# Graph network on one core: the states of the edge loops leave from ScalarE's queue, one chunk later, instead of from SyncE's

## The chip, the cores and the metric

The kernel runs on one core of a Trainium2 chip. The metric is the time of one execution on the device, in microseconds (us). Three timed runs of the kernel before took 10173.44, 10185.69 and 10188.64 us; their median is 10185.69 us.

The engines are named as in the profile: PE is TensorE, DVE is VectorE, ACT is ScalarE, POOL is GpSimd and SP is SyncE. An engine that starts DMA transfers has a queue for that; in the profile `SPq` is SyncE's queue and `ACTq` ScalarE's. The memory from which tables are read and to which results go is the chip's DRAM; the tiles that engines work on lie in SBUF, and what PE writes lies in PSUM banks of 128 x 512 fp32.

## The reference

The input is a graph of 10000 nodes with 64 features and 160000 edges with 64 features. Each edge has a source and a destination, and the edges come sorted by destination. The reference applies two networks one after the other, each to a layer norm and ReLU of x, and adds the result to x.

The first has four softmax layers. Each gives every node a softmax over its incoming edges, feature by feature:

```python
m = relu(x[src] + ea) + EPS
logits = m * t
mx = segment_max(logits, dst)
e = exp(logits - mx[dst])
agg = segment_sum(m * e / segment_sum(e, dst)[dst], dst)
h = relu(layernorm((agg + x) @ W1 + b1)) @ W2 + b2
```

Here `ea` is the edges' features times a weight, the same in all four layers. The second network is one attention layer: a score per edge and head from K of the source, Q of the destination and E of the edge, clipped and put through exp, and a sum of V times the score over each node's edges.

## The kernel before

**How the work is tiled.** The edges are split into two halves of 80000. Features lie on the partitions: 64 partitions for the first half and 64 for the second, so one tile of 128 x 512 holds 512 edges of each half. Such a tile is a *chunk*. A half has 625 groups of 128 edges; 155 chunks have four groups, and the last three have two, two and one. Each of the five edge loops has 158 chunks.

**The stages** follow one another: encoding of the nodes (to about 115 us), softmax layer 0 (to 2010), then in turns a node layer (some 170 us) and softmax layers 1, 2 and 3 (2186 to 4005, 4172 to 6000, 6165 to 8000), a last node layer, the attention layer (8310 to 10150), and the final addition.

**A softmax layer** does not compute the maximum of each node first. It runs along the edges and carries a *state*: the running maximum `u`, the running sum of the exponentials `se` and the running sum of messages times exponentials `sm`. Each chunk's `se` and `sm` are written out to the DRAM tensor `st0` for every edge, and the node layer that follows gathers the row of each node's last edge from it. Chunk k passes these steps, with the line numbers of the profile:

- `fetch`, three chunks ahead, on SP: two loads of 64 KB with the marks of where a node's edges end (L797), and one load of 256 KB with the edges' features, transposed, from `eaT` (L766). In layer 0 the features come as rows (L773, L775), PE turns them (L784, L785), ACT copies the result (L788), and SP stores it to `eaT` for the later layers (L789).
- `front`: POOL gathers the source rows in 8 gathers (L756) into one of seven buffers `xg`. PE multiplies the features by their weight (L829) and adds the gathered rows (L831) in a bank `z`. ACT writes `lg` from it (L834, L835), DVE scans for the running maximum (L841) and subtracts it (L843), and ACT makes `up` and `e` (L846, L848, L849).
- `decay`: ACT makes `dec` from `up` (L856), in a single bank.
- `back`, one chunk later: DVE makes the messages (L869) and the scans `se` (L871) and `sm` (L874), transposes both into a tile `so` (L900), of which there are three, and SP issues four stores of 128 KB from it to `st0` (L904).

In layers 1 to 3 `z` takes turns in five banks, in layer 0 in three. Layer 0 also counts edges per node on DVE and PE (L468 to L477), and layer 1 clears a buffer in DRAM with one transfer of zeros every fourth chunk (L1131, on SP).

**The attention layer** has the same form. SP loads the queries (L1141), the marks and the features two chunks ahead. POOL gathers K and V in 8 gathers (L756). PE and DVE form the scores (L1180, L1183, L1185, L1191), ACT takes the exp (L1192), PE and DVE prepare the next chunk's queries (L1151 to L1160), and DVE scans the sums (L1201) and transposes them (L1212). SP stores them to `st1` in four stores of 64 KB (L1216).

**What sets the order.** `InOrder` ties every instruction to the one before it on its engine, so each engine works in the order of the program text. In an iteration k of a softmax loop that order is: the fetch of chunk k+3, the front of chunk k, the turning of chunk k+2 (layer 0 only), the counts (layer 0), the back of chunk k-1, and the decay of chunk k. On ACT it reads: `lg`, `lg`, `up`, `e`, `e`, in layer 0 the copy `ea` of chunk k+2, then `dec`. On SP it reads: marks, marks, `ea` of chunk k+3, then the four stores of chunk k-1.

**Waits of transfers.** Transfers of SP's and ACT's queues share eight completion semaphores in turn, in the order of the program. A transfer is issued only when the one eight before it has landed. POOL's gathers have eight of their own.

Of the kernel before, what the change touches and what calls it, by code (L numbers as in the profile page):

```python
# [26 lines left out]
def kernel(ctx: ExitStack, tc: tile.TileContext, a, out):  # L27
# [10 lines left out]
    nc = tc.nc  # L38
# [760 lines left out]

    V, S = nc.vector, nc.scalar  # L800

    def softmax_layer(l, ea_rows=None):

        prev = {}
        ph = ps("hist", [P, NT]) if ea_rows is not None else None
        per = 9
        if ph is not None:
            numbers = ps("oe", [P, P])
            V.tensor_copy(numbers, iota_row)
            nc.vector.tensor_scalar_mul(teps, tcol, EPS)  # L810

        def fetch(k):
            return load_marks(k, ends_d), load_ea(k) if ea_rows is None else load_rows(k, ea_rows)

        def z_bank(k):

            if ph is None and k % 5 > 2:
                return ps(("ept", "hist")[k % 5 - 3], [P, CE])
            return ps_a([P, CE])

        def front(k, marks, ea):
            g0, n, cols = span(k)
            m = n * G
            xg = edge.tile([P, CG, 2, D], F32, name="xg", bufs=7)
            for g in range(n):
                for s in range(2):
                    gather(xg[:, g, s, :], tables[l], index(g0 + g, s))
            z = z_bank(k)
            nc.tensor.matmul(z[:, :m], eencW, ea[:, :m], start=True, stop=False)  # L829
            for g in range(n):  # L830
                nc.tensor.matmul(z[:, g * G:(g + 1) * G], xg[:, g, :, :].rearrange("p s d -> p (s d)"),  # L831
                                 ident, start=False, stop=(g == n - 1))
            lg = ps("lg", [P, CE])
            S.activation(lg[:, :m], z[:, :m], AF.Relu)  # L834
            S.activation(lg[:, :m], lg[:, :m], AF.Identity, bias=teps[:, l:l + 1],  # L835
                         scale=tcol[:, l:l + 1])

            u = edge.tile([P, CE + 1], F32, name="u")
            last = prev.get("u", neg1)
            V.tensor_copy(u[:, 0:1], last)  # L840
            V.tensor_tensor_scan(u[:, 1:m + 1], lg[:, :m], marks[:, :m], last, op0=OP.max, op1=OP.add)  # L841
            prev["u"] = u[:, m:m + 1]
            V.tensor_sub(lg[:, :m], lg[:, :m], u[:, 0:m])  # L843

            up = edge.tile([P, CE], F32, name="up")
            S.activation(up[:, :m], lg[:, :m], AF.Relu)  # L846
            e = edge.tile([P, CE], F32, name="e")
            S.activation(e[:, :m], lg[:, :m], AF.Relu, scale=-1.0)  # L848
            S.activation(e[:, :m], e[:, :m], AF.Exp, scale=-1.0)  # L849
            return z, u, up, e  # L850

        def decay(k, up):
            g0, n, cols = span(k)
            m = n * G
            dec = ps("dec", [P, CE])
            S.activation(dec[:, :m], up[:, :m], AF.Exp, scale=-1.0)  # L856
            return dec

        def history(k):
            if ph is None:  # L860
                return []
            j0, j1 = min(k * per, R * KT), min((k + 1) * per, R * KT)
            return [count(edge, ph, j, min(j + 5, j1), numbers) for j in range(j0, j1, 5)]

        def back(k, z, u, dec, e):
            g0, n, cols = span(k)
            m = n * G
            me = edge.tile([P, CE], F32, name="me", bufs=1)
            V.scalar_tensor_tensor(me[:, :m], z[:, :m], 0.0, e[:, :m], op0=OP.max, op1=OP.mult)  # L869
            se = edge.tile([P, CE], F32, name="se")  # L870
            V.tensor_tensor_scan(se[:, :m], dec[:, :m], e[:, :m], prev.get("e", zero1),  # L871
                                 op0=OP.mult, op1=OP.add)
            sm = edge.tile([P, CE], F32, name="sm")
            V.tensor_tensor_scan(sm[:, :m], dec[:, :m], me[:, :m], prev.get("m", zero1),  # L874
                                 op0=OP.mult, op1=OP.add)
            prev["e"], prev["m"] = se[:, m - 1:m], sm[:, m - 1:m]
            if k == NC - 1:

                fin = edge.tile([P, 3], F32, name="fin", bufs=1)
                V.tensor_copy(fin[:, 0:1], u[:, m:m + 1])  # L880
                V.tensor_copy(fin[:, 1:2], se[:, m - 1:m])
                V.tensor_copy(fin[:, 2:3], sm[:, m - 1:m])
                pb = ps("oe", [D, 3])
                nc.tensor.matmul(pb, ident[:, D:], fin, start=True, stop=True)
                far = edge.tile([D, 3], F32, name="far", bufs=1)
                V.tensor_copy(far, pb)
                top = edge.tile([D, 4], F32, name="top", bufs=1)
                V.tensor_add(top[:, 0:1], far[:, 0:1], bothneg[:D, :])
                V.tensor_max(top[:, 1:2], top[:, 0:1], fin[:D, 0:1])
                V.tensor_sub(top[:, 2:3], fin[:D, 0:1], top[:, 1:2])  # L890
                V.tensor_sub(top[:, 3:4], top[:, 0:1], top[:, 1:2])
                S.activation(top[:, 2:4], top[:, 2:4], AF.Exp)
                for i, t in ((1, se), (2, sm)):
                    V.tensor_mul(far[:, i:i + 1], far[:, i:i + 1], top[:, 3:4])
                    V.scalar_tensor_tensor(t[:D, m - 1:m], fin[:D, i:i + 1], top[:, 2:3],
                                           far[:, i:i + 1], op0=OP.mult, op1=OP.add)

            so = edge.tile([P, CE // 32, 2, 32], F32, name="so", bufs=3)
            for i, t in ((0, se), (1, sm)):
                V.transpose(so[:, :m // 32, i, :], t[:, :m].rearrange("p (b e) -> p b e", e=32))  # L900
            rows_out = st0[2 * g0 * G:2 * (g0 + n) * G, :].rearrange(
                "(b e s) (h x) -> s h e b x", e=32, s=2, h=2)
            for q in range(4):
                nc.sync.dma_start(rows_out[q // 2, q % 2],  # L904
                                  so[q * 32:(q + 1) * 32, :m // 32].rearrange("p b i c -> p b (i c)"))

        order = InOrder()
        def columns_of(k):
            return got[k][1] if ea_rows is None else turn_rows(k, got[k][1])

        lead = 3
        got = [fetch(k) for k in range(lead)]
        eas = [columns_of(k) for k in range(2)]
        held, counts = None, []
        for k in range(NC):
            if k + lead < NC:
                got.append(fetch(k + lead))
            z, u, up, e = front(k, got[k][0], eas[k])
            if k + 2 < NC:
                eas.append(columns_of(k + 2))  # L920
            for c in counts:
                add_counts(*c)
            if counts and counts[-1][-1] == R * KT:
                rows_of_nodes(edge, ph)
            if held is not None:
                back(k - 1, *held)
            held = z, u, decay(k, up), e
            counts = history(k)
            if ph is not None:
                if 8 <= k < 8 + len(groups):  # L930
                    encode_columns(k - 8)
                if k == 8 + len(groups):
                    fold_weights()
            if l == 1 and k % 4 == 0:
                clear_queries(k // 4)
            order()
        back(NC - 1, *held)
        order()

    def node_layer(l):  # L940
# [193 lines left out]
    def attention_layer():  # L1134
# [60 lines left out]
        def back(k, keep, pv, sc):  # L1195
            g0, n, cols = span(k)
            m = n * G
# [6 lines left out]
            if k == NC - 1:  # L1204
# [6 lines left out]
            so = edge.tile([P, CE // 32, 32], F32, name="so1", tag="so", bufs=3)  # L1211
            V.transpose(so[:, :m // 32, :], s[:, :m].rearrange("p (b e) -> p b e", e=32))  # L1212
            rows_out = st1[2 * g0 * G:2 * (g0 + n) * G, :].rearrange(
                "(b e s) (h c) -> s h e b c", e=32, s=2, h=2)
            for q in range(4):
                nc.sync.dma_start(rows_out[q // 2, q % 2], so[q * 32:(q + 1) * 32, :m // 32])  # L1216

        order = InOrder()
        got = [fetch(k) for k in range(2)]
# [2 lines left out]
        for k in range(NC):  # L1222
            kvs = fetch_kv(k)
            if k + 2 < NC:
                got.append(fetch(k + 2))
            pv, psc = scores(k, kvs, made)
            if held is not None:
                back(k - 1, *held)
            held = got[k][0], pv, weights(k, psc)
            if k + 1 < NC:  # L1230
                made = ahead(k + 1, *got[k + 1])
            order()
        back(NC - 1, *held)
        order()

    puts = []
# [69 lines left out]
```

## Time and profile before

| what | value |
| --- | --- |
| timed runs, median (lowest to highest) | 10185.69 us (10173.44 to 10188.64) |
| the profiled execution's own time | 10256.79 us |
| its span | 10254.7 us |
| granted clock of TensorE, mean | 0.629 |
| busiest engine, POOL | 6358.1 us (62%) |
| DVE | 5449.4 us (53%) |
| PE | 4014.2 us (39%) |
| ACT | 2805.0 us (27%) |
| hardware queues' transfers | 2247039 packets, 827.14 MB, 33.8% of 16 DMA engines |
| gathers' transfers | 215200 packets, 272.11 MB, 12.6% of 16 DMA engines |
| stores of the states, softmax layers | 2480 of 128 KB and a few smaller, all from SPq |
| stores of the states, attention layer | 620 of 64 KB and a few smaller, all from SPq |

The profile's page is of one profiled execution. Its first part gives the busy time of each engine, as a share of the span; instructions that issue transfers or wait on semaphores do not count as busy. Its groups of instructions give a line, an engine, an operation with the tiles it writes and reads, a count, the busy time with the mean of one in ns, and the idle time ahead of them with the instruction that ended most of it. In the view of waits a row reads: the engine and line that waited, the arrow to what it waited for, and then the total in us, the number of times and the longest. `remote` there means that the trace doesn't show who sent the release. In the timeline a row has the start, the length and the count of instructions of one kind that follow each other on an engine.

### The profile page before, as it was taken

The numbers are of one execution on the slowest core, as the hardware profiler recorded it, in microseconds if no ns is written. First come the engines' busy times: TensorE is split into PE (matmuls) and PEld (weight loads), VectorE is DVE, ScalarE is ACT, GpSimd is POOL, SyncE is SP. The second block draws the span as 40 slices with busy tenths as digits, with TensorE's granted clock in tenths as the row PEclk, the third lists the DMA queues.
The fourth block names the chain that finished last, engine by engine and source line by source line (L and its number), as shares of the span: only waits on it lengthen the run. The fifth ranks groups of instructions, "written<-read, shape, count | busy, mean of one in ns | idle before, by whom it ended". The sixth has DMA issues, their size and how long they took to land. (4 is left out here: it accounts for less than half of the span.)

```text
span 10254.7 us, 67417 instructions
## 1 busy us (share of the span) xinstructions
PE 4014.2 (39%) x15762; PEld 2685.3 (26%) x15762; DVE 5449.4 (53%) x7473; ACT 2805.0 (27%) x4803; POOL 6358.1 (62%) x6760
## 2 busy tenths in 40 slices
PE   3554445443333333433333343333333444444452
PEld 2333333222222221222222221222222233333331
DVE  3777677535555554355555543555555445545453
ACT  2333333333333333333333342333333310000000
POOL 4566666556666665566666646666666456666665
PEclk6666666665555556665666575555555667777776
DMA  3555555524555554244444433444444235555553
GB/s 89 113 125 123 123 124 123 123 59 119 125 125 129 128 124 109 62 102 105 104 104 103 105 78 71 105 105 104 103 104 106 62 92 122 125 123 126 122 128 82
DMA packets 2462634, 1103.63 MB, mean 108 GB/s; under 512 B 2039472, under 2 KB 2254438, under 8 KB 2462239
## 3 DMA queue, kind: packets, MB, share of 16 engines
q1 hardware_dynamic: 2247039, 827.14, 33.8%
q0 software_dynamic: 215200, 272.11, 12.6%
q8 instruction: 140, 2.29, 0.1%
q14 instruction: 255, 2.09, 0.1%
HBM read 626.51 MB, written 471.91 MB: 107 GB/s over the span
## 5 line engine op out<-in xcount | busy, mean ns | idle before, releaser
L756 POOL DMA_INDIRECT xg<-table,idxA x2500 | 2358.6, 943 | 1916.9 <-remote 829.7
L756 POOL DMA_INDIRECT xg<-table,idxB x2500 | 2358.8, 944 | 763.1 <-issue 761.2
L841 DVE TENSOR_TENSOR_SCAN u<-lg,u,marks 128x512 f32<-128x512 f32 (+1 forms) x628 | 798.5, 1272 | 2721.5 <-ACT lg L835 1612.7
L829 PE MATMUL z<-ea,eencW 128*128 128x512 f32 (+1 forms) x892 | 864.3, 1071 | 2137.1 <-DMA ea<-eaT 898.3
L831 PEld LDWEIGHTS z<-ident,xg 128*128 128x128 f32 x3512 | 800.4, 311 | 591.8 <-issue 566.5
L756 POOL DMA_INDIRECT kv<-kv_table,idxA x625 | 589.5, 943 | 439.7 <-remote 220.2
L831 PE MATMUL z<-ident,xg 128*128 128x128 f32 x3512 | 794.5, 395 | 162.0 <-DMA xg<-table,idxB 85.9
L829 PEld LDWEIGHTS z<-ea,eencW 128*128 128x128 f32 x892 | 222.2, 306 | 2231.8 <-issue 1981.7
L871 DVE TENSOR_TENSOR_SCAN se<-dec,se,e 128x512 f32<-128x512 f32 (+1 forms) x628 | 792.2, 1261 | 0.0
L874 DVE TENSOR_TENSOR_SCAN sm<-dec,sm,me 128x512 f32<-128x512 f32 (+1 forms) x628 | 782.3, 1246 | 0.0
L846 ACT ACTIVATE up<-lg 128x512 f32<-128x512 f32 (+1 forms) x632 | 374.3, 592 | 1352.9 <-issue 693.6
L756 POOL DMA_INDIRECT kv<-kv_table,idxB x625 | 589.7, 944 | 191.1 <-issue 190.2
L834 ACT ACTIVATE lg<-z 128x512 f32<-128x512 f32 (+1 forms) x446 | 249.4, 559 | 1555.8 <-remote 1032.3
L1185 PE MATMUL dec<-eq,head_sum 128*128 128x512 f32 (+2 forms) x316 | 237.1, 841 | 931.2 <-DVE eq L1183 887.1
L1192 ACT ACTIVATE sc<-sc 128x512 f32<-128x512 f32 (+1 forms) x158 | 98.7, 625 | 1744.7 <-DVE sc L1191 685.0
L784 PE MATMUL ept<-ident,er 128*64 128x128 f32 x1250 | 269.3, 380 | 752.4 <-ACT ea L788 517.7
L856 ACT ACTIVATE dec<-up 128x512 f32<-128x512 f32 (+1 forms) x632 | 377.1, 597 | 658.8 <-issue 561.0
L756 POOL DMA_INDIRECT n_g<-st,ends x316 | 300.8, 952 | 403.2 <-issue 142.2
L835 ACT ACTIVATE lg<-lg,teps,tcol 128x512 f32<-128x512 f32 (+1 forms) x632 | 471.4, 746 | 21.1
L829 PE MATMUL hist<-ea,eencW 128*128 128x512 f32 x186 | 189.5, 1123 | 709.5 <-DMA ea<-eaT 286.6
L829 PE MATMUL ept<-ea,eencW 128*128 128x512 f32 x186 | 185.5, 1100 | 710.3 <-DMA ea<-eaT 286.4
L1156 DVE TENSOR_TENSOR_SCAN qh<-marks,qh,oe 128x512 f32<-128x512 bf16 (+1 forms) x157 | 198.6, 1265 | 488.6 <-remote 389.8
(285 smaller groups left out, 8704.9 us busy)
## 6 DMA issues: line engine op xcount, KB each, us to landing
st<-so SPq DMA_DIRECT2D x2480, 128.0 KB
ea<-eaT SPq DMA_DIRECT2D x620, 256.0 KB
marks<-ends_d SPq DMA_DIRECT2D x1240, 64.0 KB
st<-so SPq DMA_DIRECT2D x652, 64.0 KB
xg<-table,idxA POOLq DMA_INDIRECT x2500
xg<-table,idxB POOLq DMA_INDIRECT x2500
qs<-zeros SPq DMA_DIRECT2D x40, 1000.0 KB
er<-in_edge_attr_dram SPq DMA_DIRECT2D x310, 128.0 KB
```

The costliest lines, as they stand in the source:

```text
L756: nc.gpsimd.indirect_dma_start(out=t, out_offset=None, in_=table, in_offset=bass.IndirectOffsetOnAxis(ap=idx, axis=0))
L784: nc.tensor.matmul(pt[:D, g * G:(g + 1) * G], er[:, 0, g, :], ident, start=True, stop=True)
L829: nc.tensor.matmul(z[:, :m], eencW, ea[:, :m], start=True, stop=False)
L831: nc.tensor.matmul(z[:, g * G:(g + 1) * G], xg[:, g, :, :].rearrange("p s d -> p (s d)"), ident, start=False, stop=(g == n - 1))
L834: S.activation(lg[:, :m], z[:, :m], AF.Relu)
L835: S.activation(lg[:, :m], lg[:, :m], AF.Identity, bias=teps[:, l:l + 1], scale=tcol[:, l:l + 1])
L841: V.tensor_tensor_scan(u[:, 1:m + 1], lg[:, :m], marks[:, :m], last, op0=OP.max, op1=OP.add)
L846: S.activation(up[:, :m], lg[:, :m], AF.Relu)
L856: S.activation(dec[:, :m], up[:, :m], AF.Exp, scale=-1.0)
L871: V.tensor_tensor_scan(se[:, :m], dec[:, :m], e[:, :m], prev.get("e", zero1), op0=OP.mult, op1=OP.add)
L874: V.tensor_tensor_scan(sm[:, :m], dec[:, :m], me[:, :m], prev.get("m", zero1), op0=OP.mult, op1=OP.add)
L1185: nc.tensor.matmul(psc[:, :m], head_sum, eq[:, :m], start=True, stop=True)
```

## The change

The four stores of a chunk are no longer issued in `back`. `back` puts their four pairs of destination and source on a list, `leaving`. A new function, `send_states`, takes the oldest entry from the list and issues its stores with `S.dma_start`, which is ACT's queue. In a softmax loop it is called in iteration k after the front of chunk k, the turning of chunk k+2 and the counts, and before the back of chunk k-1, so that it issues the stores of chunk k-2. In the attention loop it is called after the scores of chunk k and before the back of chunk k-1. After each loop it is called twice, before and after the last `back`.

On ACT an iteration of a softmax loop then reads: `lg`, `lg`, `up`, `e`, `e`, in layer 0 the copy `ea` of chunk k+2, the four stores of chunk k-2, `dec`. On SP it reads: marks, marks, `ea` of chunk k+3 (in layer 0 marks, marks, two loads of rows, the store to `eaT`).

```diff
+    leaving = []
+
+    def send_states():
+        for to, t in leaving.pop(0) if leaving else ():
+            S.dma_start(to, t)
+
     def softmax_layer(l, ea_rows=None):
...
             rows_out = st0[2 * g0 * G:2 * (g0 + n) * G, :].rearrange(
                 "(b e s) (h x) -> s h e b x", e=32, s=2, h=2)
-            for q in range(4):
-                nc.sync.dma_start(rows_out[q // 2, q % 2],
-                                  so[q * 32:(q + 1) * 32, :m // 32].rearrange("p b i c -> p b (i c)"))
+            leaving.append([(rows_out[q // 2, q % 2],
+                             so[q * 32:(q + 1) * 32, :m // 32].rearrange("p b i c -> p b (i c)"))
+                            for q in range(4)])
...
             if counts and counts[-1][-1] == R * KT:
                 rows_of_nodes(edge, ph)
+            send_states()
             if held is not None:
                 back(k - 1, *held)
             held = z, u, decay(k, up), e
...
+        send_states()
         back(NC - 1, *held)
+        send_states()
         order()
...
             rows_out = st1[2 * g0 * G:2 * (g0 + n) * G, :].rearrange(
                 "(b e s) (h c) -> s h e b c", e=32, s=2, h=2)
-            for q in range(4):
-                nc.sync.dma_start(rows_out[q // 2, q % 2], so[q * 32:(q + 1) * 32, :m // 32])
+            leaving.append([(rows_out[q // 2, q % 2], so[q * 32:(q + 1) * 32, :m // 32])
+                            for q in range(4)])
...
             pv, psc = scores(k, kvs, made)
+            send_states()
             if held is not None:
                 back(k - 1, *held)
...
+        send_states()
         back(NC - 1, *held)
+        send_states()
         order()
```

## The prediction

> **What bounds the kernel now.** I read the page's busy times first, then a table by stage, then the waits inside one layer, and then the timelines of the queues.
>
> ```profile
> PE 4014.2 (39%) x15762; PEld 2685.3 (26%) x15762; DVE 5449.4 (53%) x7473; ACT 2805.0 (27%) x4803; POOL 6358.1 (62%) x6760
> L756 POOL DMA_INDIRECT xg<-table,idxA x2500 | 2358.6, 943 | 1916.9 <-remote 829.7
> L841 DVE TENSOR_TENSOR_SCAN u<-lg,u,marks 128x512 f32<-128x512 f32 (+1 forms) x628 | 798.5, 1272 | 2721.5 <-ACT lg L835 1612.7
> ```
>
> No engine is full. The busiest is POOL, whose work in the edge loops is issuing gathers: one takes 0.943 us, and 1.248 us from start to start while POOL waits for nothing. A chunk of 512 edges per half needs 8, so POOL's floor is 8 x 1.248 = 9.98 us per chunk.
>
> ```profile
> 115.00:2010.00 1895.00, 905.79 (x5344) 647.54 (x5340) 1291.14 (x1901) 646.17 (x1116) 1167.54 (x1238) 0.64 0.55 119
> 4172.00:6000.00 1828.00, 581.66 (x1566) 377.96 (x1566) 966.98 (x1276) 562.47 (x949) 1179.36 (x1250) 0.60 0.44 100
> 8310.00:10150.00 1840.00, 891.28 (x4376) 660.13 (x4376) 926.67 (x1108) 98.74 (x158) 1178.51 (x1250) 0.73 0.52 123
> ```
>
> These are softmax layer 0, softmax layer 2 (1 and 3 are like it) and the attention layer: length, then busy time of PE, PE's weight loads, DVE, ACT and POOL, the granted clock, the DMA share and GB/s. Each has 158 chunks at 11.62, 11.5 and 11.36 us, start to start of DVE's first scan. So 1.4 to 1.6 us per chunk are lost over POOL's floor. In layers 1 to 3 the loss comes in a cycle of 6 chunks: 4 chunks 6.9 us apart, then two pauses of about 18 and 22.6, 68.3 us in all, with POOL idle once for 8.6 us (59.9 + 8.6 = 68.5).
>
> The waits inside layer 2 say what ends the pauses:
>
> ```profile
> DVE u L841 <- ACT lg L835: 669.5, 77, 21.8
> ACT lg L834 <- remote: 626.1, 45, 21.0
> PE z L829 <- DMA ea<-eaT: 288.4, 35, 16.7
> PE z L829 <- DMA marks<-ends_d: 229.8, 32, 9.2
> POOL xg L756 <- remote: 223.0, 26, 13.0
> ```
>
> DVE waits for ACT, ACT for PE, and PE for *loads* that SP issues (the marks row stands for the load beside it in SP's queue). The loads are asked for three chunks ahead, so they should be there. SP's timeline shows why they aren't:
>
> ```profile
> 2974.67 4.93 SPq L904 DMA_DIRECT2D st<-so  x4
> 2980.33 1.39 SPq L797 DMA_DIRECT2D marks<-ends_d  x2
> 2983.85 0.70 SPq L766 DMA_DIRECT2D ea<-eaT  x1
> 2987.36 5.75 SPq L904 DMA_DIRECT2D st<-so  x4
> ...
> 3011.34 0.84 SPq L904 DMA_DIRECT2D st<-so  x2
> ```
>
> In these layers SP is hardly ever idle. Its steps (a DMA or a wait instruction) take a median of 0.699 us with 0.7 us between them, 1.4 us a step, and a chunk has about 9: 12.6 us, more than POOL's 9.98. SP falls behind until everything stops, does 7 to 10 steps at 0.3 to 0.55 us, and falls behind again. PE's chunks then come one per load:
>
> ```profile
> 4444.44 2.04 PE L829 MATMUL z<-ea,eencW 128*128 128x512 f32 x2 [8.98 <-DMA marks<-ends_d]
> 4456.55 2.05 PE L829 MATMUL z<-ea,eencW 128*128 128x512 f32 x2 [8.74 <-DMA marks<-ends_d]
> ```
>
> The other two kinds of stage are different: there SP stands waiting for others, not others for SP.
>
> ```profile
> SPq L789 <- ACT ea L788: 566.4, 84, 30.2
> SPq L1216 <- DVE so L1212: 518.2, 44, 41.2
> ```
>
> **The change, part by part.** No instruction, byte or transfer is added or taken away: 632 stores in each of four softmax layers and 632 in the attention layer, 3160, go from SP's queue to ACT's. The order on PE, DVE and POOL stays.
>
> *SP, layers 1 to 3.* Seven DMAs per chunk become three (two marks, one ea); with their waits 9 steps become about 5, at 1.4 us 7.0 us per chunk, under POOL's 9.98. The backlog goes and the loads run up to three chunks ahead. PE, which has five banks for z in these layers, can work on several chunks whose gathers have landed. What stays is whatever makes PE's results reach ACT late: ACT's wait for PE (the remote row) lasts up to 21 us though PE's recorded work had ended. When POOL runs out of its 7 gather buffers the chain restarts 7 to 8 us after the last gather landed in layers 1 to 3, but about 2 us after it in layer 0 (1031.6 us) and in attention (9026 us), where SP has no backlog. So of POOL's 8.6 us of idleness per 6 chunks, 8.6 - 5.1 = 3.5 stay if all the difference in restart goes, and 6 if half of it does: cadence (59.9 + 3.5)/6 = 10.57 to (59.9 + 6)/6 = 10.98, against 11.52. Gain 0.54 to 0.95 us x 474 chunks = 255 to 450 us; I take 350.
>
> *SP, layer 0 and attention.* 9 DMAs become 5, and 8 become 4, in a queue on which nobody waits: the cover is SP's own idle time, above 500 us per stage. 0, with 50 us either way.
>
> *ACT, layers 1 to 3.* The four stores stand between e and dec of the same chunk, in a queue that runs in order. They wait for a transpose two chunks old, done long before. In a fast stretch a chunk takes 6.91 us, of which ACT stands 1.21 before dec; the stores fill that first, so the loop becomes 6.91 - 1.21 + S = 5.7 + S, S being the time of four stores. Behind them stand dec and the next chunk's lg, and DVE waits for both. The trace has no DMA from ACT's queue, so S is bounded by SP's rows: from below by its fast stretches, 2.2 to 2.4 us (2.40 at 1303.94 in layer 0), from above by its slow ones, 5 us plus a gap and a wait step, 5.6 to 7. The loop is 8.0 us by the one, under POOL's floor and free; by the other 11.3 to 12.7. I take the lower: ACT's own instructions in the same stretches run back to back (0.60, 0.59, 0.63 us), with no sign of SP's 0.7-us beat, and ACT would have one queue's stores only. Cost 0, up to (12.7 - 11.5) x 474 = 570 us.
>
> *A wait that moves.* A DMA waits until the eighth before it has landed, over both queues. In layers 1 to 3 there are 7 per chunk, so the first store of a chunk waits for the previous iteration's ea load. The trace has that row for SP (SP's stores wait for ea<-eaT: 107.2 us, 83 times, 1.3 us each). On ACT it would hold dec and lg behind a load two chunks ahead. With SP ahead it has landed; with SP late it adds 83 x 1.3 = 107 us per layer at most. I take 0.
>
> *ACT, layer 0 and attention.* In layer 0 the stores (2.3 us) come after up, e, e and the ea copy; DVE sets a fast chunk there at 8.3 us, so ACT has room, and POOL's floor lies above. In attention ACT is busy 98.7 of 1840 us, and its exp mostly waits for DVE. 0 in both; without that cover 158 x 2.3 = 363 us per stage.
>
> *One chunk later.* The tile of states has three buffers; keeping one a chunk longer leaves DVE's transpose waiting for a store issued a whole chunk (10 us) before, and stores land in 2.2 to 2.8 us. 0. The last chunk's stores still go out at once, so the 53 us that the node layer waits for the last states stay.
>
> *Two rules of the Trainium skill against it.* "DMA: Bandwidth & Descriptors", section "Issuing engines are not separate DMA queues", says that DMAs from any engine run on the same 16 DMA engines, and that spreading the issue saves only sequencer time, "usually small relative to the DMA itself". By it the sum would be about 0. The row says that here the sequencer's time is not small: 12.6 us of steps per chunk, while the DMA engines are busy 44% and a store lands within 2.8 us. But the skill has a point: if SP's slow steps come from what the transfers meet farther on, their number per chunk is unchanged. "Perfetto Trace Analysis", section "DMA Instruction — HWDGE (DVE, Sync)", says that the profiled time of such an issue includes waiting for a descriptor generator that sequencers share. By it ACT would stand behind SP's three DMAs at worst, 3 x 0.55 = 1.65 us: the loop is 9.7, still under 9.98. No run here shows two queues issuing at once.
>
> The profiled execution took 10256.79 us (span 10254.7), 0.7% above the median of 10185.69; gains are worked out in its time and taken off the median: 10186 - 350 = 9836, say 9840.
>
> **The rivals.**
> (A) As above, 9840; 9735 to 9930 by its own terms, with layer 0 and attention 9690 to 9980.
> (B) POOL becomes the bound in layers 1 to 3: 9.98 to 10.1 us per chunk, 1.4 to 1.54 x 474 = 660 to 730 less, 9455 to 9525. For it: all that POOL lacks is freed buffers. Against it: PE's late results, which the change doesn't touch.
> (C) The change doesn't do what it says: loads still come late, since what paces SP is met by every DMA and semaphore. For it: three kinds of stage with quite different queues all run at 11.4 to 11.6 us, and layer 0 is not faster for SP being free. Against it: PE's waits for loads exist in layers 1 to 3 only, and the restart there is 5 us longer. 10185, within 60 or so.
> (D) Slower: the slow beat follows the stores to ACT. Place: between e and dec; price: loop 5.7 + S; it decides from S = 5.8 us, 1.45 us per store, where the loop is 11.5; from 4.3 us (1.07 each) it eats the gain. At S = 6.3 the loop is 12.0: +0.5 x 474 = 237, 10425; at worst 10186 + 570 = 10756. For it: SP's beat was of that size for the same DMAs. Against it: layer 0 issues them in 2.2 to 2.4 us beside the same gathers.
>
> **How the numbers follow.** Chances: A 0.44, B 0.10, C 0.20, D 0.26. 0.2% (20 us) is about what a measurement of this kernel can tell from no change; of C, 0.08 falls within it, 0.07 below and 0.05 above. Faster: 0.44 + 0.10 + 0.07 = 0.61; same 0.08; slower 0.26 + 0.05 = 0.31. The likeliest is A, 9840, with its own range of 9690 to 9980. Since cases of both signs matter, the range runs from the upper end of B, 9520 (leaving out about 0.06), to the middle of D, 10430 (leaving out about 0.12).
>
> **What would show it.** Right: in layers 1 to 3 the waits of PE for ea and marks, 518 us in layer 2, fall below 150; SP waits for buffers instead of working; ACT's four stores take 2.2 to 2.6 us before dec; POOL's share rises from 62% to 64% or more; the gain lies in layers 1 to 3, with layer 0 and attention within 25 us each. Wrong: stores of 1.4 us on ACT with DVE's scan waiting for them (D); a wait of ACT's stores for ea loads (the moved wait); PE's waits for loads the same with SP mostly idle (C).

## The result, and the profile after

The changed kernel takes 10223.69 us (median of six runs, 10206.69 to 10232.98), the kernel before 10186.06 (six runs, 10173.44 to 10191.26): ratio 1.0037, 95% interval 1.0027 to 1.0048. It is slower by 0.37%, some 38 us, where I forecast 9840 us.

One thing must be known to read what follows: the same program does not take the same time on every chip. Here, and on chip 15 of the experiments, the kernel before takes 10168 to 10186 us; on chips 2, 3, 7 and 10 it takes 8758 to 8780. I call them slow and quick chips, and give each time of the experiments beside that of the kernel before on the same chip; the chip of the result's runs is not on record.

The page of after, first line and the stores' row, with ACT's queue in SP's place:

```profile
PE 4160.5 (41%) x15762; PEld 2741.2 (27%) x15762; DVE 5450.9 (53%) x7473; ACT 2808.6 (27%) x4803; POOL 6374.5 (62%) x6760
...
st<-so ACTq DMA_DIRECT2D x2480, 128.0 KB
```

POOL's share is 62% as before. Softmax layer 2 by its length, busy times (PE, weight loads, DVE, ACT, POOL), clock, DMA share and GB/s is nearly the row of before, but for PE's busy time (582 before) and the granted clock (0.60 before):

```profile
4172.00:6000.00 1828.00, 628.96 (x1566) 393.38 (x1566) 966.98 (x1276) 563.33 (x949) 1184.35 (x1253) 0.55 0.44 101
```

The waits inside that layer, of after, first the engines' and then SP's queue's:

```profile
DVE u L847 <- ACT lg L841: 685.3, 72, 21.8
...
ACT lg L840 <- remote: 292.6, 32, 20.6
...
ACT dec L862 <- DMA st<-so: 205.7, 53, 7.3
```

```profile
SPq L766 <- remote: 345.7, 31, 25.9
SPq L797 <- DVE u L847: 144.9, 30, 6.2
SPq L766 <- PE z L837: 108.0, 11, 25.2
```

What the change set out to do, it did. PE's waits for `ea` and `marks`, 518 us of this layer before in the rows of the tile `z` alone, are gone from the list, and SP, which was hardly ever idle, now stands waiting for buffers. Yet DVE still waits 685 us for ACT (669 before). Measured from the trace, start to start of DVE's first scan, in us per chunk:

| stage | before | after |
| --- | --- | --- |
| softmax layer 0 | 11.62 | 11.55 |
| softmax layers 1, 2, 3 | 11.53, 11.49, 11.49 | 11.51, 11.47, 11.45 |
| attention | 11.36 | 11.31 |

The profiled execution of before (10256.79 us) lies above all its timed runs and that of after (10232.98) does not, so the pair of traces shows where time is spent, but cannot divide the 0.37%.

Where the expected gain went is seen in one pause of after, on ACT, PE and POOL (the last column is the idle time before and what ended it):

```profile
4475.26 0.60 ACT L862 ACTIVATE dec<-up 128x512 f32<-128x512 f32 x1 [4.60 <-DMA st<-so]
4492.06 0.58 ACT L840 ACTIVATE lg<-z 128x512 f32<-128x512 f32 x1 [16.20 <-remote]
```

```profile
4443.03 2.08 PE L835 MATMUL z<-ea,eencW 128*128 128x512 f32 x2 [3.73 <-DVE lg L849]
4444.90 1.91 PE L837 MATMUL z<-ident,xg 128*128 128x128 f32 x8
...
4475.25 0.37 PE L837 MATMUL z<-ident,xg 128*128 128x128 f32 x1 [2.43 <-issue]
4478.05 0.37 PE L837 MATMUL z<-ident,xg 128*128 128x128 f32 x1 [2.42 <-DMA xg<-table,idxB]
```

```profile
4485.46 0.95 POOL L756 DMA_INDIRECT xg<-table,idxB  x1 [0.30 <-issue]
4492.30 0.95 POOL L756 DMA_INDIRECT xg<-table,idxA  x1 [5.89 <-remote]
```

By the order of the banks, the `lg` that starts at 4492.06 reads the chunk that PE worked on at 4443: its matmuls are recorded as done at 4446.8, and ACT got them 45 us later, once POOL had run out of its seven buffers and stopped. Meanwhile PE, three chunks further, does a matmul pass every 2.1 to 2.8 us, and but for one gather the profile shows nothing that it waits for. Taken over layer 2, the time from the recorded end of a chunk's last matmul to the start of its `lg` is 9 to 31 us before (5th to 95th percentile, median 19.4) and 22 to 53 us after (median 32.6). On a quick chip it is 0.0 us for either kernel: `lg` starts at the recorded end, which is modelled. So the loads now come early and PE works earlier, but its results are delivered no earlier.

POOL's stops in these layers end with that delivery. Count as a stop an idle time of more than 1.5 us ahead of a chunk's first gather, from a layer's ninth chunk on: layers 1 to 3 have 83 before, 675 us in all, and 113 after, 633 us; on the quick chip's traces there are none. All 83, and 112 of the 113, end 0.24 us after ACT starts `lg` on the chunk whose buffer POOL needs, seven chunks back (4492.06 and 4492.30 above): both had been waiting for PE's work on that chunk. In layer 2 the 26 stops of 8.7 us (median) became 39 of 5.0, shorter but more. The rows of POOL's waits there, after (223.0 us in 26 times before; short ones are counted in):

```profile
POOL xg L756 <- remote: 75.4, 23, 6.6
POOL xg L756 <- PE z L837: 69.6, 12, 9.9
POOL xg L756 <- PE hist L837: 40.2, 7, 12.7
POOL xg L756 <- PE ept L837: 30.5, 5, 9.9
```

The row of `dec` waiting for `st<-so` is for a good part a wait for a load. In layer 2 the first store of 32 of the chunks starts only after `e` has ended, 110 us in all, and 2.6 to 3.4 us after SP has issued an `ea` load. By the order of the semaphores that load is the transfer eight before the store (SP, then ACT):

```profile
4470.36 0.33 SPq L766 DMA_DIRECT2D ea<-eaT  x1
```

```profile
4470.03 0.63 ACT L855 ACTIVATE e<-e 128x512 f32<-128x512 f32 x1
4473.21 2.00 ACTq L806 DMA_DIRECT2D st<-so  x4
```

### The profile page after: what moved, and what is told of

The parts are those of the page before. It is cut to its first block, busy times and chain, and to the rows that moved or that the text cites. A ratio compares the mean times of both kernels' runs of the same rounds, so it can differ in the third digit from the quotient of the medians.

```text
span 10231.0 us, 66928 instructions
## 1 busy us (share of the span) xinstructions
PE 4160.5 (41%) x15762; PEld 2741.2 (27%) x15762; DVE 5450.9 (53%) x7473; ACT 2808.6 (27%) x4803; POOL 6374.5 (62%) x6760
## 4 chain that ended last, share of the span: by engine, by line
POOL 26%; issue 24%; another core or an unknown queue 18%; ACT 9%; PE 9%; DVE 8%; DMA 3%; ACTq 3%; SPq 1%; DVEq 0%; POOLq 0%
POOL xg L756 25%; ACTq L806 3%; ACT lg L841 2%; DVE u L847 2%; PE dec L1194 1%; PE z L1189 1%; PE oe L1160 1%; ACT up L852 1%; ACT dec L862 1%; ACT lg L840 1%; ACT e L854 1%; PE z L837 1%; DMA st<-so 1%; ACT e L855 1%
## 5 line engine op out<-in xcount | busy, mean ns | idle before, releaser
L835 PE MATMUL z<-ea,eencW 128*128 128x512 f32 (+1 forms) x892 | 886.9, 1097 | 1262.3 <-DMA xg<-table,idxB 420.6
L837 PE MATMUL z<-ident,xg 128*128 128x128 f32 x3512 | 866.6, 393 | 845.7 <-issue 702.6
L837 PEld LDWEIGHTS z<-ident,xg 128*128 128x128 f32 x3512 | 831.6, 308 | 1291.3 <-issue 1221.9
L849 DVE TENSOR_TENSOR lg<-lg,u 128x512 f32<-128x512 f32 (+1 forms) x632 | 438.2, 693 | 21.9
L784 PEld LDWEIGHTS ept<-ident,er 128*64 128x64 f32 x1250 | 216.7, 201 | 830.5 <-ACT ea L788 680.5
```

Source lines behind the costliest of these rows:

```text
L784: nc.tensor.matmul(pt[:D, g * G:(g + 1) * G], er[:, 0, g, :], ident, start=True, stop=True)
```

## The experiments

Three theories were set against each other. **T1**: on the slow chips a queue works in a slow beat while POOL streams gathers; before, SP was the queue that was late, now it is PE. **T2**: the stores' transfers are what everything meets, whichever queue issues them. **T3**: the stores in ACT's order took back what SP gave. The traces of the result bear on T3: in layer 2 ACT's standing ahead of `lg` fell from 720 to 497 us, and that ahead of `dec` rose from 189 to 408. But where POOL's stops end, ACT had been standing ahead of `lg`, for PE, so the stores in its order did not hold POOL there. The first four runs were on a quick chip.

**A quarter of the stores, on ACT (e1, and f3 and g3).**

```diff
-                            for q in range(4)])
+                            for q in range(4 if ea_rows is not None else 1)])
```

> The changed kernel with one of the four stores of each chunk in softmax layers 1 to 3; three quarters of the states there are not written, so later results are not the reference's. Theory T1 (SP's queue was only one victim: while POOL's gathers stream, a queue works at a beat of one step in 1.4 us; with SP freed, PE is the queue that is late): ACT's chain gets 1.7 us shorter and 1536 packets per chunk go, but the cadence of layers 1 to 3 stays at 11.3 to 11.6 us. Theory T2 (the transfers of the stores are what everything meets, whichever queue issues them): cadence falls to 10.0 to 10.6 us, 430 to 700 us in all. Theory T3 (the stores in ACT's order took back what SP gave): cadence falls to 10.0 to 10.6 us as well, with the waits of dec for the stores (207 us in layer 2) gone.

8774.48 us, against 8758.49 for the kernel before on that chip; 9.91 to 9.92 us per chunk in layers 1 to 3. Two repeats ran on quick chips too:

> The changed kernel with one of four stores in layers 1 to 3, as once before (three quarters of the states aren't written), for the slow beat. With the beat: 10.0 to 10.8 us per chunk if the stores' transfers (1536 packets of 256 bytes less) make the beat (T2), 11.2 to 11.6 if not. Without the beat: 9.91 us, as before.

> The changed kernel with one of four stores in layers 1 to 3 (three quarters of the states aren't written). Without the beat it ran at 9.90 us. With the beat: 10.0 to 10.8 if the stores' transfers make the beat (T2), 11.2 to 11.6 if not.

8762.09 and 8762.07 us (before: 8780.01 and 8762.32), 9.90 us per chunk. These are single runs, 0.18% above, 0.20% below and level with the kernel before, and the cadence stays: on a quick chip neither the stores' number nor their bytes set the pace. For the slow beat these runs say nothing.

**Half of PE's gathered rows (e2, d2).**

```diff
-            for g in range(n):
+            for g in range(n) if ea_rows is not None else sorted({0, n - 1}):
                 nc.tensor.matmul(z[:, g * G:(g + 1) * G], xg[:, g, :, :].rearrange("p s d -> p (s d)"),
```

> The changed kernel with PE adding only two of a chunk's four groups of gathered rows in layers 1 to 3 (the first and the last; the others are left out of the sum): 12 instead of 20 weight loads and matmul passes per chunk, with all gathers and stores as they were. T1: a chunk in PE's slow beat takes 12 x 1.4 = 17 instead of 28 us, POOL stands less, cadence of layers 1 to 3 falls from 11.5 to 10.0 to 10.8 us (330 to 700 us in all). T2 and T3: PE's number of steps is not the matter, cadence 11.4 to 11.6 us.

On the quick chip 8773.10 us (before 8758.49), 9.91 us per chunk: POOL's pace. The same kernel reached a slow chip later:

> The changed kernel with PE adding only two of a chunk's four groups of gathered rows in layers 1 to 3 (the others are left out of the sum), as once before, in case this chip has the slow beat. With the beat: 10.0 to 10.8 us per chunk if PE's number of steps now holds the loop (T1), 11.4 to 11.6 if the transfers do (T2). Without the beat: 9.91 us, as before, since POOL sets the pace.

10202.64 us, before 10167.68; 11.47, 11.36 and 11.43 us per chunk. The beat itself is as T1 has it: in slow stretches the scans are 16.8 us apart (16.1 to 17.5), where the full number of steps gave up to 28.0, and 12/20 of 28 is 16.8. But the mean is only 0.03 to 0.11 us below that of after on the slow chip of the result, and POOL's stops, 612 us in all, still end with PE's delivery (109 of 113). So PE's number of steps does not set the pace, and T1 in that form falls; 8 weight loads and matmul passes less per chunk bought nothing, as four DMAs less on SP had bought nothing.

**Four buffers of gathered rows instead of seven (e3).**

```diff
-            xg = edge.tile([P, CG, 2, D], F32, name="xg", bufs=7)
+            xg = edge.tile([P, CG, 2, D], F32, name="xg", bufs=4)
```

> The changed kernel with 4 instead of 7 buffers for gathered rows (attention: 4 instead of 7 half-chunks). T1: POOL runs less far ahead, the cycle gets shorter and the pauses come more often; if the share of time that must be paused is fixed, cadence of layers 1 to 3 stays 11.4 to 11.8 us; if each pause has a fixed cost, it rises above 12.5 us. T2: fewer gathers in flight change nothing in the packets, 11.4 to 11.6 us.

(The diff shows the first of three places; the two other tiles that share these buffers change alike.) 8790.43 us, 9.93 us per chunk, on the quick chip: POOL hardly runs ahead there. It tells nothing of the slow beat.

**A memset on POOL after each chunk's gathers (e4).**

```diff
+            if ea_rows is None:
+                nc.gpsimd.memset(pace, 0.0)
```

> The changed kernel with one memset of 128 x 1024 on POOL (0.94 us) after each chunk's gathers in layers 1 to 3, which makes POOL's floor about 11.0 us per chunk. T1, if POOL must merely be away from gathering for some time per chunk: the memset takes the place of the pauses, cadence 11.0 to 11.6 us. If the memset is not such a pause, or only the gathers' landing counts: pauses stay and the cadence is 12.4 us or more. T2: 11.4 to 11.6 us, as POOL has 1.5 us per chunk to spare.

9173.13 us; layers 1 to 3 at 10.75 us, the others at 9.84 and 9.93. On a quick chip POOL's floor is the pace, and the memset (0.97 us in its trace) adds 0.83 us per chunk. The slow beat was not tested with it.

**Both kernels on one quick chip, and the two halves of the change apart (b1, a1, a2, a3).**

> The kernel before once more, on the chip of this call, for its trace. The four experiments ran on a chip where the kernel before took 8758 us, not 10186: no slow beat there, and all five edge loops at POOL's floor. If this chip is like that: 158 chunks at 9.84 to 9.93 us in every stage, SP's stores at 0.55 us, no waits of PE for ea loads. If it is like the first one: 11.4 to 11.6 us.

> The changed kernel on the same chip. T1 (the loss over POOL's floor is a slow beat that befalls the queues on the first chip, and the change only moves it): without the beat POOL sets the pace with either queue, so the change is worth nothing in the loops and the ratio is 0.998 to 1.005, any loss lying where a loop ends. T3 (ACT's chain is longer with the stores): loop 5.7 + 2.3 = 8.0 us is still under 9.98, so the same. A ratio above 1.01 would be against both.

> The changed kernel with the stores one chunk later, but from SP's queue: the delay without the queue. If what the change costs lies at the end of the loops (the last states leave later, and the node layer's gathers wait for them), the ratio is that of the changed kernel within 0.1%; if it lies in ACT's order, this one is at 1.000 within 0.1%.

```diff
-            S.dma_start(to, t)
+            nc.sync.dma_start(to, t)
```

> The kernel before with the stores from ACT's queue and no delay: the queue without the delay. ACT then waits for the transposes of the chunk before (me, se, sm and two transposes, 0.68 + 1.27 + 1.26 + 0.69 + 0.67 = 4.6 us after the subtraction), issues 2.3 us of stores and only then dec: loop 0.55 + 0.75 + 1.28 + 0.70 + 4.6 + 2.3 + 0.6 = 10.8 us in layers 1 to 3, above POOL's 9.98. Expected 0.8 x 474 = 380 us and something in layer 0: ratio 1.03 to 1.06 where POOL's floor rules. If the delay is not needed, 1.000 to 1.005.

```diff
-                nc.sync.dma_start(rows_out[q // 2, q % 2],
+                nc.scalar.dma_start(rows_out[q // 2, q % 2],
                                   so[q * 32:(q + 1) * 32, :m // 32].rearrange("p b i c -> p b (i c)"))
```

| kernel, on one quick chip | us | ratio to before (95%) | us per chunk, layers 1 to 3 |
| --- | --- | --- | --- |
| before | 8762.10 | 1 | 9.90 |
| after | 8773.77 | 1.0014 (1.0007 to 1.0020) | 9.91 |
| one chunk later, on SP | 8762.42 | 1.0000 (0.9992 to 1.0009) | 9.90 |
| at once, on ACT | 9136.96 | 1.0428 (1.0411 to 1.0446) | 10.40, 10.33, 10.34 |

The delay costs nothing; ACT's queue costs 12 us, and without the delay 375, of which some 150 lie in layer 0 (10.81 us per chunk, 9.87 before). Without it ACT waits for the transposes of the chunk before, 2.4 us of its 4.64 us of standing, and only then issues (timeline of ACT, stores at once on ACT):

```profile
4602.65 0.63 ACT L849 ACTIVATE e<-e 128x512 f32<-128x512 f32 x1
4605.68 2.19 ACTq L904 DMA_DIRECT2D st<-so  x4
4607.92 0.60 ACT L856 ACTIVATE dec<-up 128x512 f32<-128x512 f32 x1 [4.64 <-DMA st<-so]
```

The 12 us of after lie where a layer ends. From the last gather of layer 1 to the first of the node layer POOL stands 17.93 us before and 20.81 after. The two kernels on the quick chip, before and then after:

```profile
3374.18 0.95 POOL L756 DMA_INDIRECT xg<-table,idxB  x1 [0.30 <-issue]
3393.05 0.94 POOL L756 DMA_INDIRECT n_g<-st,ends  x1 [17.93 <-DMA marks<-ends_d]
```

```profile
3376.87 0.94 POOL L756 DMA_INDIRECT xg<-table,idxB  x1 [0.30 <-issue]
3398.62 0.94 POOL L756 DMA_INDIRECT n_g<-st,ends  x1 [20.81 <-DMA st<-so]
```

Over the four layers it is 4.3, 2.9, 3.0 and 3.0 us more, 13.2 in this pair of traces, where the medians are 11.7 apart. In the last chunks nothing more is gathered, so the chain of DVE and ACT is the pace there, and in it stand ACT's stores: in a chunk of two groups they take 2.15 us before a `dec` that reads half as much.

**The tail back on SP (c1), and two stores on each queue (c2).**

```diff
+            send_states(S if k < NC - 6 else nc.sync)
...
-        for to, t in leaving.pop(0) if leaving else ():
-            S.dma_start(to, t)
+        for q, (to, t) in enumerate(leaving.pop(0) if leaving else ()):
+            (S if q < 2 else nc.sync).dma_start(to, t)
```

(The first line is c1, the rest c2. In c1 the queue is an argument of `send_states`, and the two calls after the loop take SP's.)

> The changed kernel with the stores of the last chunks of each softmax layer (from iteration 152 of 158 on) issued by SP again. If what the change costs, where POOL sets the pace, is that at a layer's end ACT has four stores in each of the last chunks' chains (2.5 to 3 us per layer between the last gather and the last scan), it goes back to 1.000, within 0.05%, against 1.0014. If the cost is in the loops or in what is gathered first by the node layer, it stays at 1.001 or more. On a chip with the slow beat: 1.002 to 1.004, as the loops are not changed.

> The changed kernel with two of a chunk's four stores from ACT and two from SP, one chunk later. ACT's 1.1 us then lie wholly in its 1.21 us of waiting before dec, so the loop stays 6.9 us. Where POOL sets the pace: 1.000 to 1.0005. On a chip with the slow beat: if SP's number of steps were what holds the loop (my forecast), SP's 7 instead of 9 steps take 9.8 us and the ratio is 0.95 to 0.98; if the beat goes to whichever queue is late (T1), 0.998 to 1.005.

c1: 8763.16 us, 1.0002 (0.9994 to 1.0011); c2: 8761.33 us, 0.9999 (0.9991 to 1.0008); before 8761.80. Taking ACT's stores out of the last chunks removes the loss, so its place on a quick chip is shown. Two stores on ACT cost nothing measurable. Neither beats the kernel before on a quick chip, and neither was tried on a slow one.

**Each store twice, on ACT (d1), on a slow chip.**

```diff
+    st_x = dram.tile([2 * HALF + 1, D2], F32, name="st_x")
...
-            rows_out = st0[2 * g0 * G:2 * (g0 + n) * G, :].rearrange(
-                "(b e s) (h x) -> s h e b x", e=32, s=2, h=2)
+            outs = [t[2 * g0 * G:2 * (g0 + n) * G, :].rearrange(
+                "(b e s) (h x) -> s h e b x", e=32, s=2, h=2) for t in ((st0, st_x) if l else (st0,))]
...
-                            for q in range(4)])
+                            for rows_out in outs for q in range(4)])
```

> The changed kernel with each store of layers 1 to 3 issued twice from ACT, the second time to a tensor of DRAM that nobody reads: eight stores per chunk, which tests the loop 5.7 + S of the forecast. S = 8 x 0.55 = 4.4 us, loop 10.1 us against POOL's 9.98: where POOL sets the pace the cadence of layers 1 to 3 goes from 9.91 to 10.1 to 10.4 us, 90 to 230 us in all. If ACT can issue stores beside its other work, or DVE's side has more slack than I saw, it stays at 9.91. If the doubled transfers themselves weigh, above 10.6 us.

10362.96 us, before 10167.68. ACT's issue in the loop of this kernel:

```profile
5003.40 0.63 ACT L856 ACTIVATE e<-e 128x512 f32<-128x512 f32 x1
5003.40 2.36 ACTq L807 DMA_DIRECT2D st<-so  x4
5005.80 2.65 ACTq L807 DMA_DIRECT2D st_x<-so  x4
5008.50 0.60 ACT L863 ACTIVATE dec<-up 128x512 f32<-128x512 f32 x1 [4.47 <-DMA st<-so]
```

In layer 2 half of the chunks are 10.3 to 10.6 us apart, where the forecast's 5.7 + S with S of 5.0 gives 10.7. The layers' means are 11.80, 11.69 and 11.69, only 0.2 to 0.3 above those of the changed kernel on the slow chip of the result. Doubling the stores adds 2048 packets per chunk (the layer moved 144 GB/s, not 101) and 2.7 us of ACT's time, and most of that vanishes in time that POOL would have stood anyway: its stops are 662 us in all (after: 633), and its gathers last no longer than before, 1767 to 1773 us a layer. What the doubling costs stands mostly at the layers' ends, where POOL waits 91 to 107 us for the last states (after: 60 to 65). That speaks against T2 and against T3 as what makes the loss.

**Half of the gathers, with the stores on ACT and on SP (f1, f2, and g1, g2).**

```diff
+            step = 1 if ea_rows is not None else 2
-            for g in range(n):
+            for g in range(0, n, step):
...
-                nc.tensor.matmul(z[:, g * G:(g + 1) * G], xg[:, g, :, :].rearrange("p s d -> p (s d)"),
+                nc.tensor.matmul(z[:, g * G:(g + 1) * G], xg[:, g - g % step, :, :].rearrange("p s d -> p (s d)"),
```

> The changed kernel with only the gathers of the first and third group of each chunk in layers 1 to 3 (four instead of eight; the other two groups add the rows of their neighbour, so the sums are wrong). POOL's floor becomes 5.0 us. On a chip without the slow beat the loop of DVE and ACT sets the pace: 5.7 + 2.3 = 8.0 us by the forecast, 7.4 to 8.2, from 9.91. With the beat: if what is lost over POOL's floor is lost to the gathers (T1), 7.4 to 8.5 us; if it is a fixed pace or the stores' transfers (T2), 11.3 to 11.6.

> The kernel before with the same half of the gathers. Without the beat: 6.9 us, DVE's and ACT's loop without the stores, 0.5 to 1.1 us less than the changed kernel, which is the price of the stores on ACT where POOL doesn't hide it. With the beat: if SP's slow steps hold this kernel as the forecast had it, 11 us or more (9 steps of 1.4 us), against 7.4 to 8.5 for the changed one; if SP's steps are slow only while POOL streams, 6.9 to 8.

On a quick chip: 7653.73 us with the stores on ACT (7.86, 7.42, 7.39 us per chunk), 7329.94 with them on SP (6.87 in all three). With POOL out of the way SP issues all seven DMAs of a chunk in 6.87 us, and the change costs 324 us, 0.68 us per chunk. ACT, first with the stores on its queue, then with them on SP:

```profile
3301.36 0.63 ACT L856 ACTIVATE e<-e 128x512 f32<-128x512 f32 x1
3301.37 2.43 ACTq L806 DMA_DIRECT2D st<-so  x4
3303.85 0.60 ACT L863 ACTIVATE dec<-up 128x512 f32<-128x512 f32 x1 [1.85 <-DMA st<-so]
```

```profile
3302.69 0.63 ACT L850 ACTIVATE e<-e 128x512 f32<-128x512 f32 x1
3304.53 0.60 ACT L857 ACTIVATE dec<-up 128x512 f32<-128x512 f32 x1 [1.21 <-DVE sm L875]
```

The pair ran once more, on another quick chip:

> The changed kernel with four instead of eight gathers per chunk in layers 1 to 3, again (two groups add their neighbour's rows). Without the beat it ran at 7.4 us there. With the beat: 7.4 to 8.5 us if the loss is the gathers' (T1), 11.3 to 11.6 if it is a fixed pace or the transfers' (T2); in between, if POOL is paused by what its gathers do to the other queues and has half as much to pause for, 8 to 9.5.

> The kernel before with the same half of the gathers. Without the beat it ran at 6.87 us in layers 1 to 3. With the beat: 11 us or more if SP's slow steps hold it for themselves, as the forecast had it; 6.9 to 8.5 if SP is slow only while POOL streams.

7651.99 and 7331.15 us, before 8762.32: the same to 2 us. On a slow chip the pair was not run.

## Why the prediction was wrong

**What bounds the kernel.** That no engine was full, that POOL's floor lay at 9.98 us and 1.4 to 1.6 us per chunk were lost over it was right; on the quick chips the five loops of the kernel before run at 9.82 to 9.90 us, the short last chunks included. That SP was always busy in layers 1 to 3, one step in 1.4 us, was in the trace, and so were PE's waits for loads. But that SP's lateness *caused* the loss was inferred from who waited for whom. What POOL's stops ended with was another thing, PE's delivery.

**SP, layers 1 to 3: the step that failed.** The term was: of POOL's 8.6 us of idleness per 6 chunks only 3.5 to 6 stay, 255 to 450 us gained. Measured in layer 2, POOL's gathers last 1774.4 us before and 1764.1 after, over 1250 x 1.248 = 1560: lost per chunk 1.36 us and 1.29. The term is about 0.07 x 158 = 10 us per layer, and the longer end of the layer takes most of that back (last gather to last scan 43.5 us before, 49.7 after). I had read the 7 to 8 us from POOL's stop to the restart, against 2 elsewhere, as the price of the backlog, and had held the number of stops at one per 6 chunks. The stops did get shorter, from 8.7 to 5.0 us, but there were 39 instead of 26 in the layer. The trace of before had the warning: layer 0, without the backlog, stops 99 times for 2.8 us (median), 315 us in all, more than layer 2 with its 223. What restarts the chain is PE's delivery, which I named as "what stays" and then let shrink with the backlog. Its size was to be read from the trace of before: 9 to 31 us from PE's recorded end to `lg` in nine of ten chunks of layer 2, not only in the pauses. With loads early, PE ends earlier and that time grows to 22 to 53.

**ACT's cost.** Right in kind and above its size: S is 2.2 to 2.4 us as taken from SP's quick rows, and the slow beat did not follow the stores to ACT (2.34 and 2.35 us in the slow chip's profile of after, at 4443.54 and 4451.01; median 2.31 in layer 2, nineteen of twenty under 2.6). The wait behind SP's DMAs, priced at up to 1.65 us, does not show in that. The loop 5.7 + S = 8.0 was measured as 7.4, because the first store is issued beside the last `e`, not after it (3301.37 and 3301.36 above): 0.6 us too much. Where POOL hides it the cost is 0 as forecast. But the cover was said to be POOL's floor all through the loop, and at the loop's end there is no POOL: on the quick chip 2.9 to 4.3 us per layer, 12 us by the medians, were left out. The 53 us that the node layer waits for the last states were said to stay; in the slow chips' traces they are 60 to 65 after.

**The wait that moves** was put at 0, because with SP ahead the load would have landed. It came all the same, 110 us in layer 2, about the 107 named as the most: SP is no longer behind, but now has to wait for buffers before it can load. That it cost little was luck. ACT waits for PE right after, and only 3 us of it in layer 2, 6 in layer 3 and 22 in layer 1 go beyond that wait.

**One chunk later** was right at 0: the delay alone is 1.0000. The delay is also what makes ACT's queue bearable (1.0014 with it, 1.0428 without); there the loop is 10.4 us where the sum gave 10.8.

**The rivals.** C is what came, "the change doesn't do what it says", in its outcome though not in its reason: the loads do come early. What I listed for it was the best evidence in the text: three kinds of stage with quite different queues ran at the same 11.4 to 11.6 us. B and D did not come. The Trainium skill's rule in "DMA: Bandwidth & Descriptors", section "Issuing engines are not separate DMA queues", that spreading the issue saves only sequencer time, would have given about 0, which agrees with the measured 1.0014 and 1.0037, and was nearer than my reading of the row. The row was true, but of a queue that did not set the pace.

**What stays open.** What delays PE's results and stretches its and SP's steps to a beat of 0.7 and 1.4 us on the slow chips. It is not the number of SP's DMAs (after), nor that of PE's steps (d2), nor mainly the stores' transfers (d1, twice as many for 0.2 to 0.3 us), nor slower transfers or a lower granted clock (see the last section). That it is tied to POOL's streaming of gathers is an inference: results arrive after POOL has stopped, but POOL stops for want of them; half of the gathers, the test for it, ran on no slow chip. That the chip itself makes a run slow or quick is inferred too: no chip was seen both ways, but only chip 10 served in two sets of runs.

Of the 0.37%, the 12 us at the ends of the layers were shown on a quick chip. On the slow pair of traces POOL stands there 53 to 55 us before and 60 to 65 after, 33.5 us more over the four layers: seven or eight chunks are still to be finished when it stops, on a quick chip two, and each full one takes 7.4 instead of 6.9 us. That could be most of the 38 us. It is not shown, since each side is one profiled execution, the loops' gathers are 10 to 19 us a layer shorter in the same pair, and if the two kernels' runs were on different chips, part of the difference may be the chips' (10168 and 10186 us for the kernel before).

## What to carry to other kernels

A queue that is always busy and has someone waiting for it is not yet the pace: ask whether stages without that queue run at another cadence, and if they don't, look for what they have in common before pricing the gain. A stop that gets shorter may come more often, so forecast the sum of the stops and not the length of one. When transfers move to the queue of an engine that computes, find where the cover ends, usually in the last chunks of a loop, and delay them until their data is long ready, or that engine takes over the wait. Moving only half of them may keep within its idle time (c2).

## What the runs showed of the hardware that I had not expected

- The same program took 8758 to 8780 us on some chips and 10168 to 10186 on others, with gathers of the same length (0.943 to 0.946 us) and the same work. For the kernel before, the granted clock was 0.629 on a slow and 0.619 on a quick chip, and SyncE's transfers kept the 16 DMA engines busy for 33.8% of 10254.7 us and 39.5% of 8761.7 us, which is the same 3466 and 3461 us: neither tells the chips apart. On the slow one ACT starts on a bank 9 to 31 us after PE's recorded end (layer 2), on the quick one at once.
- On a slow chip a late queue's steps fall on a beat: with PE late, chunks come up to 28 us apart with 20 weight loads and passes, 16.8 with 12, that is 1.4 us each; SP takes the same 1.4 us a step before. ACT's and DVE's computing showed no such beat.
- A DMA issue of ACT starts 0.01 us after the start of the activation ahead of it in program order and runs beside it, so that four stores of 2.4 us delay what follows by 1.85 us only.
- Stores moved to ACT's queue can still be held by SP's loads, through the completion semaphores that the two queues share: 32 times in layer 2 of after, 110 us.
